# Seven products of halves from block 2 on, with the weights' sums formed in place in block 0's FFN

## The chip, the cores and the metric

The kernel runs on one core of a Trainium2 chip. The metric is the device time of one execution in microseconds (us). Every time below without a unit is in us. Engines: PE is TensorE, DVE VectorE, ACT ScalarE, POOL GpSimd, SP the engine whose queue issues nearly all DMAs.

## The reference

Input x has 4 sequences of 1024 tokens with 512 features. Two layers follow each other, each with a residual and layer norms on both sides:

```
h   = layernorm(x)
q, v, g = h @ Wq.T, h @ Wv.T, silu(h @ Wg.T)          # 512 x 512 each
ret_t = lam * ret_(t-1) + v_t                           # scan over the tokens, lam per head
x   = x + layernorm((layernorm(q * ret) * gamma + beta) * g @ Wo.T)
h   = layernorm(x)
f   = silu(h @ fp8(gate_w) * gate_s) * (h @ fp8(up_w) * up_s)   # 512 -> 1536
x   = x + layernorm(f @ fp8(down_w) * down_s)                   # 1536 -> 512
```

fp8() rounds a weight to float8 e4m3 and back. Everything else is float32. A weight beyond 448 would become a NaN in the reference; the kernel searches for such weights and passes a NaN on if there is one.

## The kernel before, in words

The 4096 tokens are cut into 8 blocks of 512 (NB = 8, TB = 512). Each block goes through a retention part (class Retention) and an FFN part (class Ffn). The two are interleaved: the main loop `for t in range(NB)` runs block t's FFN in NI = 12 steps i. Step i multiplies for the gate (pfg) and for up (pfu), each 8 float32r matmuls of 128x512, forms the fused value, and adds the down product (pd) of step i - 2. Between these groups stand pieces of the retention part of block b = t + 1 and, late in the loop, the first projections of block n = t + 2. At step 11 block n's projections begin; the document calls that place a turn. In the code `a`, `b`, `n` are the retention objects of blocks t, t + 1, t + 2, and `l` is the FFN of block t - 1, whose output norms are finished during this FFN.

The order of the work on each engine is the order of the program text: the wrapper InOrder keeps every instruction in program order on its engine. All instructions are recorded at one line (L74), so groups are told apart by tile names. SP's queue is in order too: a DMA whose input is not ready holds those behind it.

There are two ways to project. Up to block 2 (FAST = 3) the projection is direct: for each of 4 output chunks, 4 matmuls of 128x512 in float32 (pv, pq, pg from wv_sb, wq_sb, wg_sb). A float32 matmul leaves two records in the trace. From block 3 on it is done with seven products of halves (Strassen's scheme): for each of v, q, g seven products of a 256x256 weight quarter (or a sum of quarters) with 256 features of 256 tokens, each 4 matmuls of 128x256 (method product). They need sums of the weight's quarters (operands 5, 6, 7, 3) and sums of the input's quarters (t_sums, formed by input_sums on POOL). The weight operands are fetched from DRAM for each product into w_ring, a ring of 4. The partial results are kept in mids. The three tiles w_ring, t_sums and mids take over the space of wq_sb, wv_sb and wg_sb.

The sums of the weights' quarters are formed in weight_sums on DVE, 12 additions of 128x512 into tiles of the pool work ("tok"), and stored to DRAM by SP (dsum_v, dsum_q, dsum_g), during steps 0 and 1 of block 1's FFN.

Late in each FFN (i = 7 to 11) block b's retention output is finished per slice s of 128 tokens: o (matmul po), o_moments (DVE statistics, POOL reciprocal root), x1_of (normalised x1n, POOL adds it to x, SP stores it as kept), x1_moments, x1n_of, and then the transposed copy x1nT: for s = 0 to 2 by move_x1n, a DVE transpose by blocks and two DMA legs through DRAM (mxs, x1n), and for s = 3 by turn_x1n on TensorE (pt). upper_of (ACT) and rest_of (DVE) write the two halves of x1nT that the next FFN multiplies. For blocks 0 and 1 x1n is computed by ACT (shift_scale), from block 2 on by DVE (center_scale).

The search for weights over 448 (find_over, tile seen) is 24 ACT passes of 128x1536, spread over the steps of block 1's FFN by the list look. Its result is combined in pass_over, with a matmul (over_all) on TensorE, in step 1 of block 2's FFN.

PSUM: pf has two banks for pfg and pfu in turn, pa0 and pa1 serve the retention part, pd0 to pd3 the down sums.

Of the kernel before, what the change touches and what calls it, by code (L numbers as in the profile page):

```python
# [23 lines left out]
def retention_ffn_sandwich(  # L24
# [203 lines left out]
    def find_over():  # L228


        k = 0
        for j in range(4):
            for w in (gate_sb, up_sb, down_sb):
                v = w[:, ts(j, NI // 4), :] if w is down_sb else w[:, :, ts(j, I // 4)]
                for sign in (1.0, -1.0):
                    tag = "ret" if k >= 6 else "xn"
                    seen = work.tile(list(v.shape), F8, tag=tag, name=f"seen_{k}", bufs=2 if k >= 6 else 1)
                    act.activation(
                        seen, v.bitcast(F32), AF.Relu, bias=neg_max, scale=sign,
                        accum_out=over[:, k : k + 1], saturate=False,  # L240
                    )
                    k += 1
                    yield
# [3 lines left out]
    def pass_over():  # L247

        dve.reduce_sum(total, over, mybir.AxisListType.X)
        po = ps_tile("over_all")  # L250
        pe.matmul(po[:, :1], mean_w, total, start=True, stop=True)
        dve.tensor_scalar(total, po[:, :1], 3e38, 3e38, ALU.mult, ALU.mult)
        dve.tensor_scalar(total, total, 0.0, None, ALU.mult)
        dve.tensor_scalar(ds_sb, ds_sb, total, None, ALU.add)


# [72 lines left out]

    FAST = 3  # L330
    H = TB // 2
# [3 lines left out]
    banks = {"v": {1: 0, 6: 1, 5: 0}, "q": {1: 1, 6: 0, 5: 1}, "g": {1: 0, 6: 0, 5: 1}}  # L335
    squares = {"v": (wvT, wv_sb), "q": (wqT, wq_sb), "g": (wgT, lambda: wg_sb)}
    operands = {}

    def weight_sums():

        for k, (src, w) in squares.items():
            w = w() if callable(w) else w
            v = src.rearrange("(c p) f -> p c f", p=P)
            a11, a12, a21, a22 = (w[:, i : i + 2, o : o + H] for o in (0, H) for i in (0, 2))
            operands[k] = {1: v[:, 0:2, 0:H], 2: v[:, 2:4, 0:H], 4: v[:, 2:4, H:D]}
            done = {}
            for j, x, y, op in (
                (5, a21, a22, ALU.add), (6, 5, a11, ALU.subtract),
                (7, a11, a21, ALU.subtract), (3, a12, 6, ALU.subtract),
            ):  # L350
                t = work.tile([P, D], F32, tag="tok", name=f"sum_{k}{j}", bufs=4)
                done[j] = t.rearrange("p (c f) -> p c f", c=2)
                x, y = (done[o] if isinstance(o, int) else o for o in (x, y))
                dve.tensor_tensor(done[j], x, y, op)
                operands[k][j] = dram.tile([P, 2, H], F32, tag=f"sum_{k}{j}", name=f"dsum_{k}{j}", bufs=1)
                sp.dma_start(operands[k][j], done[j])
                yield

    sums = weight_sums()
    RING = 4  # L360
# [478 lines left out]
    for n in range(4):  # L839
        load_piece(n)  # L840
    wg_sb = load_square(wgT, "wg_sb")
    a = Retention(0, x_first)
    a.new_xnT()
# [126 lines left out]

    look = [2, 2, 2, 0, 1, 3, 3, 3, 2, 2, 2, 2]
    l = None
    for t in range(NB):
        f, n = Ffn(a), None
        fast = b is not None and b.fast
        for i in range(NI):
            if t > 0 and (t > 1 or i):
                (f if i else l).rest((i - 1) % NI)
            if t == 0 and i == 0:
                n = Retention(2)  # L980
                rounds(3, now=False)

            if l and i == 0:
                l.fetch()
# [3 lines left out]
            if l and not b and i == 3:  # L988
                for s in range(NS // 2, NS):
                    l.scale(s)  # L990
            if l and b and not fast and i == 3:
                l.norm(0)
                l.add(0)
                l.norm(1)
                l.add(1)
            if l and not b and i in (6, 7):
# [7 lines left out]
            if n and i == 6 and t > 0:  # L1004
                n.stats(2)
                n.stats(3)
                n.rstd()
                if n.fast:
                    n.shift()
            if b and not fast and i == 5:  # L1010
                b.z(0)
            if b and i >= 8:
                b.x1_moments(i - 8)
            f.gate(i)
            if t == 0 and i in (5, 6):
# [5 lines left out]
            if fast and i in (0, 1, 2, 3, 4, 5, 6):  # L1021
                b.product()
            if fast and i == 2:
                l.stats(0)
# [6 lines left out]
            if b and t == 0 and i < 2:  # L1031
                b.q(i + 2, tokens=slice(None) if i else later)
                b.y_of(i + 2)
            if b and not fast and t > 0 and i < 3:
                b.v(i + 1)
                b.scan(i + 1)
            if l and b and not fast and i == 2:
                l.stats(0)
                l.stats(1)
            if b and not fast and i == 3:  # L1040
                b.halves()
                units()
                if t == 0:
                    rounds(3, now=False)
                b.g_of(0)
                b.mean()
                b.center_y()
                if t == 0:
                    n.stats(3)
                    n.rstd()  # L1050
                    n.shift()
            if b and not fast and i == 4:
                b.halves()
                if t == 0:
                    rounds(3, now=False)
                b.g_of(1)
                b.var()
# [3 lines left out]
            if b and not fast and i == 6:  # L1061
                b.g_of(3)
                b.z(2)
                if t == 0:
                    b.z(3)
            if b and 7 <= i <= 10:
# [9 lines left out]
            if b and 7 <= i <= 10:  # L1076
                b.o_moments(i - 7)
            if n and n.fast and i == 11:
                n.input_sums(1, 2)
            units()  # L1080
            f.up(i)
            f.fuse(i)
            if b and not fast and i == 4:
                b.rstd_y()
            if n and i == 11:
                if n.fast:
                    n.products(2)
                else:
                    n.v(0)
                    n.scan(0)  # L1090
                b.turn_x1n(3, "pf")
                b.upper_of(3)
            if fast and i < 6:
                b.product()
            if fast and i == 2:
# [25 lines left out]

            if l and b and not fast and i == 2:
                l.stats(2)
                l.stats(3)
                l.rstd()
# [5 lines left out]
            if l and b and not fast and i == 3:  # L1131
                l.norm(2)
                l.add(2)
                l.norm(3)
                l.add(3)
            if b and not fast and t > 0 and i < 3:
                b.q(i + 1)
                b.y_of(i + 1)
            if b and not fast and i == 6 and t > 0:
                b.z(3)  # L1140
            if n and i == 5 and t == 1:
                n.stats(0)
                n.stats(1)
            if n and i == 6:
# [5 lines left out]
            if n and t > 0 and 6 <= i <= 9:  # L1150
                n.norm_x(i - 6, n.fast)
                n.send_x(i - 6)
# [5 lines left out]
            if b and n and i == 11:  # L1158
                b.rest_of(3)
            if n and i == 11:  # L1160
                if n.fast:
                    n.product()
                    n.input_sums(3, 4)
                else:
                    n.q(0)
                    n.y_of(0)

# [19 lines left out]
            if fast and i == 4:  # L1187
                b.product()
                b.var()
                b.rstd_y()  # L1190
            if n and n.fast and i == 11:
                n.product()
            if n and t > 1 and i == 5:
                n.stats(0)
                n.stats(1)
            if t == 1 and i < 2:
                for _ in range(6):
                    next(sums, None)
            if t == 1 and i == 6:
                t_sums = wpool.tile([P, 4, 2, H], F32, tag="wv_sb", name="t_sums")  # L1200
                w_ring = wpool.tile([P, RING, 2, H], F32, tag="wq_sb", name="w_ring")
                mids = wpool.tile([P, 4, 2, H], F32, tag="wg_sb", name="mids")
                for _ in range(RING):
                    fetch_weights()
            if b and i == 4 and 0 < t < NB - 2:
                n = Retention(t + 2)
            if t == 2 and i == 1:
                pass_over()
            if t == 2 and i == 4:
# [72 lines left out]
```

## Time and profile before

| what | value |
|---|---|
| runs, median of 3 | 992.82 (991.87 to 992.85) |
| the profiled execution | 991.89, span 990.1, granted TensorE clock 0.998 |
| PE busy | 968.6, 98% of the span |
| DVE busy | 657.1, 66% |
| ACT busy | 365.3, 37% |
| POOL busy | 256.4, 26% |
| DMA | 104.56 MB, 106 GB/s in the mean |
| stage of block 0's FFN (95.21 to 201.26) | DVE 80.98, ACT 59.91, DMA share 0.37 at 105 GB/s |
| stage of block 1's FFN (201.26 to 326.04), block 2 direct | PE 122.32 of 124.78, DVE 81.71, ACT 67.05 |
| stage of block 3's FFN (446.03 to 564.80), block 4 by products | PE 117.66 of 118.77, DVE 78.56, ACT 33.95 |

A row of the timeline holds the start, the duration, the engine, the line, the operation, output tile <- input tiles, the shape, how many instructions are merged, and in brackets the idle time of the engine before it with what ended it. A row of the list of waits holds who waited for whom, the sum in us, how many times, and the longest. Matmuls are pipelined and their ends are modelled, so that the distance of two starts is the surer measure.

### The profile page before, as it was taken

How to read it: one execution, taken by the hardware profiler on the slowest of the kernel's cores; microseconds unless marked ns; L12 is line 12 of the kernel's file. 1: busy time of each engine (PE TensorE's matmuls, PEld its weight loads, DVE VectorE, ACT ScalarE, POOL GpSimd, SP SyncE). 2: the span in 40 equal slices, each digit the busy share in tenths (PEclk: the TensorE clock that was granted, in tenths of full speed). 3: DMA queues.
4: the chain of work that ended last, by engine and by line, in shares of the span. 5: the costliest groups of instructions: out<-in, count | busy, mean ns of one | idle time of the engine just before them, and what ended most of it. 6: DMA issues, size and time to landing. Idle time of an engine off the chain costs nothing.

```text
span 990.1 us, 11037 instructions
## 1 busy us (share of the span) xinstructions
PE 968.6 (98%) x3878; PEld 722.0 (73%) x3878; DVE 657.1 (66%) x1006; ACT 365.3 (37%) x549; POOL 256.4 (26%) x337
## 2 busy tenths in 40 slices
PE   9999999999999999999999999999999999999996
PEld 7455766666666878678876788767887788877885
DVE  5996978548746567665686566866567656756445
ACT  3556575433765125221432114321152211512223
POOL 1405121203314033240513305132141312322020
PEclk9999999999999999999999999999999999999999
DMA  9312314412136326253243633245241542213021
GB/s 295 119 64 73 119 64 104 130 64 85 65 98 149 126 69 229 80 144 118 85 128 90 160 91 109 94 129 157 76 149 57 136 138 75 75 32 117 0 86 43
DMA packets 85223, 104.56 MB, mean 106 GB/s; under 512 B 7728, under 2 KB 49712, under 8 KB 85168
## 3 DMA queue, kind: packets, MB, share of 16 engines
q1 hardware_dynamic: 83584, 102.92, 34.5%
q10 hardware_dynamic: 1584, 0.94, 0.5%
q8 instruction: 31, 0.51, 0.2%
q14 instruction: 24, 0.20, 0.1%
HBM read 71.06 MB, written 32.77 MB: 105 GB/s over the span
## 4 chain that ended last, share of the span: by engine, by line
PE 86%; DVE 6%; POOL 3%; ACT 2%; issue 1%; DMA 1%; ACTq 0%; DVEq 0%; SPq 0%; POOLq 0%
PE pfu L74 16%; PE pfg L74 16%; PE pd L74 15%; PE pv L74 10%; PE pg L74 10%; PE pq L74 9%; PE po L74 9%; POOL t_sums L74 1%; DVE st L74 1%; DVE fuse L74 1%; POOL mv L74 1%; DVE scr L74 1%; ACT seen L74 1%; POOL x L74 1%; DVE d L74 1%
## 5 line engine op out<-in xcount | busy, mean ns | idle before, releaser
L74 PE MATMUL pfu<-x1nT,up_sb 128*128 128x512 f32 x768 | 212.1, 418 | 0.0
L74 PE MATMUL pfg<-x1nT,gate_sb 128*128 128x512 f32 x768 | 194.3, 395 | 0.4 <-DVE x1nT L74 0.4
L74 PE MATMUL pd<-down_sb,fuse 128*128 128x512 f32 x720 | 187.2, 401 | 0.0
L74 PEld LDWEIGHTS pfu<-x1nT,up_sb 128*128 128x128 f32 x768 | 144.5, 188 | 44.4 <-issue 14.4
L74 PEld LDWEIGHTS pfg<-x1nT,gate_sb 128*128 128x128 f32 x768 | 144.1, 188 | 30.4 <-DVE x1nT L74 0.8
L74 PEld LDWEIGHTS pd<-down_sb,fuse 128*128 128x128 f32 x720 | 135.3, 188 | 29.3 <-issue 1.7
L74 ACT CAST fuse<-gate 128x512 fp32r<-128x512 f32 x90 | 55.7, 618 | 236.4 <-DVE gate L74 236.4
L74 ACT ACTIVATE gate<-pfg,gs_sb 128x512 f32<-128x512 f32 x96 | 65.7, 684 | 206.2 <-PE pfg L74 206.1
L74 DVE SCALAR_TENSOR_TENSOR gate<-pfu,us_sb,gate 128x512 f32<-128x512 f32 x96 | 71.6, 746 | 82.8 <-PE pfu L74 82.8
L74 PE MATMUL po<-wo_sb,y 128*128 128x512 f32 x256 | 114.5, 592 | 0.0
L74 POOL TENSOR_SCALAR mv<-mv 128x1 f32<-128x1 f32 (+1 forms) x82 | 18.6, 226 | 302.6 <-DVE mv L74 301.6
L74 PEld LDWEIGHTS po<-wo_sb,y 128*128 128x128 f32 x256 | 48.2, 189 | 50.3 <-issue 46.9
L74 DVE TENSOR_TENSOR fuse<-gate,fuse 128x512 fp32r<-128x512 f32 x90 | 75.6, 840 | 9.1 <-ACT fuse L74 9.1
L74 POOL TENSOR_TENSOR ysum<-y 128x256 f32<-128x256 f32 (+1 forms) x13 | 13.5, 1038 | 188.8 <-DVE y L74 161.1
L74 POOL TENSOR_TENSOR x<-x,x1n 128x512 f32<-128x512 f32 x32 | 46.7, 1460 | 45.7 <-DVE x1n L74 36.7
L74 DVE BATCH_NORM_STATS2 st<-x 128x6 f32<-128x512 f32 x64 | 43.6, 681 | 13.7 <-POOL x L74 11.2
L74 DVE TENSOR_TENSOR mids<-pv,mids 128x512 f32<-128x512 f32 x25 | 17.3, 691 | 46.3 <-PE pv L74 43.4
L74 POOL TENSOR_TENSOR mv<-mv,nhalf 128x1 f32<-128x1 f32 (+1 forms) x75 | 45.3, 604 | 6.2
L74 PE MATMUL pv<-xnT,wv_sb 128*128 128x512 f32 (+1 forms) x120 | 42.9, 508 | 1.6 <-ACT xnT L74 1.6
L74 PE MATMUL pv<-t_sums,w_ring 128*128 128x256 f32 x160 | 38.3, 382 | 5.6 <-POOL t_sums L74 5.6
L74 PE MATMUL pq<-xnT,wq_sb 128*128 128x512 f32 (+1 forms) x112 | 43.4, 531 | 0.0
L74 PE MATMUL pg<-xnT,wg_sb 128*128 128x512 f32 x96 | 43.0, 592 | 0.0
(156 smaller groups left out, 1334.5 us busy)
## 6 DMA issues: line engine op xcount, KB each, us to landing
kept<-x SPq DMA_DIRECT2D x32, 256.0 KB, 2.1
x<-kept SPq DMA_DIRECT2D x32, 256.0 KB, 3.7
x<-in_x SPq DMA_DIRECT2D x28, 256.0 KB, 4.1
out<-d SPq DMA_DIRECT2D x27, 256.0 KB, 2.0
xnT<-mx SPq DMA_DIRECT2D x24, 256.0 KB, 4.8
mxs<-xs SPq DMA_DIRECT2D x84, 64.0 KB, 1.8
x1n<-mxs SPq DMA_DIRECT2D x21, 256.0 KB, 2.7
mx<-xn SPq DMA_DIRECT2D x20, 256.0 KB, 2.3
```

Of the source, the lines that this page charges most:

```text
L74: return lambda *args, **kwargs: tc.keep_in_program_order(op(*args, **kwargs))
```

## The change

FAST goes from 3 to 2: block 2 too is projected by seven products. All branches for direct blocks beyond block 1 go away.

The weights' sums are formed earlier and in place. At steps 8, 9 and 10 of block 0's FFN, just ahead of the gate group, DVE makes four additions in wv_sb, then wq_sb, then wg_sb, where the sums overwrite the quarters; at the end of the same step SP stores the four sums. w_ring now takes wv_sb's space and is filled at the end of step 9; t_sums and mids take the others after step 10.

At a turn input_sums forms all four input sums at once before the up group. The products there were 1 and 6, then the transposes, then 2, pd, 7; now they are 1, the transposes, pd, then 6 and 2. Product 7 moves behind the next FFN's first gate group, and step 1 has one product more.

The search runs five passes in steps 0 and 1, four in step 2, two in step 3, none in steps 4 to 6, two in steps 7 to 10 and none in step 11. Its output tile is "xn" for the first 16 passes, "ret" for the others. pass_over becomes a generator of three parts, all in step 0 of block 2's FFN: the sum on DVE ahead of the gate group, the matmul after the first product, the rest on DVE after the up group.

```diff
-                    tag = "ret" if k >= 6 else "xn"
+                    tag = "ret" if k >= 16 else "xn"
...
         dve.reduce_sum(total, over, mybir.AxisListType.X)
-        po = ps_tile("over_all")
+        yield
+        po = ps_tile("over_all", "pa0")
         pe.matmul(po[:, :1], mean_w, total, start=True, stop=True)
+        yield
...
-    FAST = 3
+    FAST = 2
...
+    def weight_sums(k):
+
+        src, w = squares[k]
+        v = src.rearrange("(c p) f -> p c f", p=P)
+        a11, a12, a21, a22 = (w[:, i : i + 2, o : o + H] for o in (0, H) for i in (0, 2))
+        operands[k] = {1: v[:, 0:2, 0:H], 2: v[:, 2:4, 0:H], 4: v[:, 2:4, H:D]}
+        dve.tensor_tensor(a22, a21, a22, ALU.add)
+        dve.tensor_tensor(a21, a11, a21, ALU.subtract)
+        dve.tensor_tensor(a11, a22, a11, ALU.subtract)
+        dve.tensor_tensor(a12, a12, a11, ALU.subtract)
+        return {5: a22, 7: a21, 6: a11, 3: a12}
+
+    def keep_sums(k, done):
+        for j, t in done.items():
+            operands[k][j] = dram.tile([P, 2, H], F32, tag=f"sum_{k}{j}", name=f"dsum_{k}{j}", bufs=1)
+            sp.dma_start(operands[k][j], t)
+
...
-    look = [2, 2, 2, 0, 1, 3, 3, 3, 2, 2, 2, 2]
+    look = [5, 5, 4, 2, 0, 0, 0, 2, 2, 2, 2, 0]
...
+            if t == 2 and i == 0:
+                next(passing)
...
+            if t == 0 and 8 <= i < 11:
+                done = weight_sums("vqg"[i - 8])
             f.gate(i)
...
-            if n and n.fast and i == 11:
-                n.input_sums(1, 2)
+            if n and i == 11:
+                n.input_sums(1, 2, 3, 4)
             units()
             f.up(i)
             f.fuse(i)
...
             if n and i == 11:
-                if n.fast:
-                    n.products(2)
-                else:
-                    n.v(0)
-                    n.scan(0)
+                n.product()
                 b.turn_x1n(3, "pf")
                 b.upper_of(3)
+            if t == 2 and i == 0:
+                next(passing)
             if fast and i < 6:
-                b.product()
+                b.products(2 if i == 1 else 1)
...
+            if t == 0 and 8 <= i < 11:
+                keep_sums("vqg"[i - 8], done)
...
-            if n and n.fast and i == 11:
-                n.product()
+            if n and i == 11:
+                n.products(2)
...
-            if t == 1 and i < 2:
-                for _ in range(6):
-                    next(sums, None)
-            if t == 1 and i == 6:
-                t_sums = wpool.tile([P, 4, 2, H], F32, tag="wv_sb", name="t_sums")
-                w_ring = wpool.tile([P, RING, 2, H], F32, tag="wq_sb", name="w_ring")
-                mids = wpool.tile([P, 4, 2, H], F32, tag="wg_sb", name="mids")
+            if t == 0 and i == 9:
+                w_ring = wpool.tile([P, RING, 2, H], F32, tag="wv_sb", name="w_ring")
                 for _ in range(RING):
                     fetch_weights()
+            if t == 0 and i == 10:
+                t_sums = wpool.tile([P, 4, 2, H], F32, tag="wq_sb", name="t_sums")
+                mids = wpool.tile([P, 4, 2, H], F32, tag="wg_sb", name="mids")
...
-            if t == 2 and i == 1:
-                pass_over()
```

More of the change, by code (lines that the diff above doesn't have):

```diff
@@ L235, in find_over @@
                 for sign in (1.0, -1.0):
-                    tag = "ret" if k >= 6 else "xn"
-                    seen = work.tile(list(v.shape), F8, tag=tag, name=f"seen_{k}", bufs=2 if k >= 6 else 1)
+                    tag = "ret" if k >= 16 else "xn"
+                    seen = work.tile(list(v.shape), F8, tag=tag, name=f"seen_{k}", bufs=2 if k >= 16 else 1)
                     act.activation(
@@ L254, in pass_over @@
         dve.tensor_scalar(ds_sb, ds_sb, total, None, ALU.add)
+        yield
+    passing = pass_over()
     def stats(src, mv):
@@ L335, in retention_ffn_sandwich @@
     banks = {"v": {1: 0, 6: 1, 5: 0}, "q": {1: 1, 6: 0, 5: 1}, "g": {1: 0, 6: 0, 5: 1}}
-    squares = {"v": (wvT, wv_sb), "q": (wqT, wq_sb), "g": (wgT, lambda: wg_sb)}
+    squares = {"v": (wvT, wv_sb), "q": (wqT, wq_sb)}
     operands = {}
[L339 to L359, printed above, removed]
+    def weight_sums(k):
[12 more added lines that the diff above has]
+            sp.dma_start(operands[k][j], t)
     RING = 4
@@ L841, in retention_ffn_sandwich @@
     wg_sb = load_square(wgT, "wg_sb")
+    squares["g"] = wgT, wg_sb
     a = Retention(0, x_first)
@@ L990, in retention_ffn_sandwich @@
                     l.scale(s)
[L991 to L995, printed above, removed]
             if l and not b and i in (6, 7):
@@ L1007, in retention_ffn_sandwich @@
                 n.rstd()
-                if n.fast:
-                    n.shift()
+                n.shift()
             if b and not fast and i == 5:
@@ L1033, in retention_ffn_sandwich @@
                 b.y_of(i + 2)
[L1034 to L1039, printed above, removed]
             if b and not fast and i == 3:
@@ L1042, in retention_ffn_sandwich @@
                 units()
-                if t == 0:
-                    rounds(3, now=False)
+                rounds(3, now=False)
                 b.g_of(0)
@@ L1047, in retention_ffn_sandwich @@
                 b.center_y()
[L1048 to L1051, printed above, removed]
+                n.stats(3)
+                n.rstd()
+                n.shift()
             if b and not fast and i == 4:
                 b.halves()
-                if t == 0:
-                    rounds(3, now=False)
+                rounds(3, now=False)
                 b.g_of(1)
@@ L1063, in retention_ffn_sandwich @@
                 b.z(2)
-                if t == 0:
-                    b.z(3)
+                b.z(3)
             if b and 7 <= i <= 10:
@@ L1082, in retention_ffn_sandwich @@
             f.fuse(i)
-            if b and not fast and i == 4:
+            if t == 0 and i == 4:
                 b.rstd_y()
             if n and i == 11:
-                if n.fast:
-                    n.products(2)
-                else:
-                    n.v(0)
-                    n.scan(0)
+                n.product()
                 b.turn_x1n(3, "pf")
                 b.upper_of(3)
+            if t == 2 and i == 0:
+                next(passing)
             if fast and i < 6:
-                b.product()
+                b.products(2 if i == 1 else 1)
             if fast and i == 2:
@@ L1120, in retention_ffn_sandwich @@
                 next(search)
[L1122 to L1125, printed above, removed]
             if l and not b and i in (4, 5):
@@ L1130, in retention_ffn_sandwich @@
                     l.rstd()
[L1131 to L1143, printed above, removed]
             if n and i == 6:
@@ L1150, in retention_ffn_sandwich @@
             if n and t > 0 and 6 <= i <= 9:
-                n.norm_x(i - 6, n.fast)
+                n.norm_x(i - 6, True)
                 n.send_x(i - 6)
@@ L1159, in retention_ffn_sandwich @@
                 b.rest_of(3)
-            if n and i == 11:
-                if n.fast:
-                    n.product()
[L1163 to L1166, printed above, removed]
+            if t == 0 and 8 <= i < 11:
+                keep_sums("vqg"[i - 8], done)
             if i == f.lag:
@@ L1190, in retention_ffn_sandwich @@
                 b.rstd_y()
-            if n and n.fast and i == 11:
-                n.product()
-            if n and t > 1 and i == 5:
+            if n and i == 11:
+                n.products(2)
+            if n and t > 0 and i == 5:
                 n.stats(0)
                 n.stats(1)
-            if t == 1 and i < 2:
-                for _ in range(6):
-                    next(sums, None)
-            if t == 1 and i == 6:
-                t_sums = wpool.tile([P, 4, 2, H], F32, tag="wv_sb", name="t_sums")
-                w_ring = wpool.tile([P, RING, 2, H], F32, tag="wq_sb", name="w_ring")
-                mids = wpool.tile([P, 4, 2, H], F32, tag="wg_sb", name="mids")
+            if t == 0 and i == 9:
+                w_ring = wpool.tile([P, RING, 2, H], F32, tag="wv_sb", name="w_ring")
                 for _ in range(RING):
                     fetch_weights()
+            if t == 0 and i == 10:
+                t_sums = wpool.tile([P, 4, 2, H], F32, tag="wq_sb", name="t_sums")
+                mids = wpool.tile([P, 4, 2, H], F32, tag="wg_sb", name="mids")
             if b and i == 4 and 0 < t < NB - 2:
                 n = Retention(t + 2)
-            if t == 2 and i == 1:
-                pass_over()
             if t == 2 and i == 4:
```

## The prediction

> **What bounds the kernel now.** I read the page's shares first, then TensorE's list of waits, then the timeline around the points that the change touches. TensorE (PE) is busy nearly all the time; the other engines are not.
>
> ```profile
> PE   968.6 (98%) x3878; PEld 722.0 (73%) x3878; DVE 657.1 (66%) x1006; ACT 365.3 (37%) x549; POOL 256.4 (26%) x337
> ```
>
> So time is won in two ways only: fewer TensorE cycles, or a shorter wait of TensorE. The longest waits in its list:
>
> ```profile
> PE pv L74 <- POOL t_sums L74: 5.6, 5, 1.1
> ...
> PE pv L74 <- DMA mxs<-xs: 1.3, 1, 1.3
> ...
> PE over_all L74 <- DVE total L74: 1.0, 1, 1.0
> ```
>
> All three are touched. The timeline gives the price of the two ways to project. A direct output chunk (8 records of 128x512 f32) and then the same of block 2's stage, and two seven-product steps of a later block:
>
> ```profile
> 203.08 3.59 PE L74 MATMUL pv<-xnT,wv_sb 128*128 128x512 f32 x8
> 206.11 2.39 PE L74 MATMUL pfu<-x1nT,up_sb 128*128 128x512 f32 x8
> 208.34 3.59 PE L74 MATMUL pq<-xnT,wq_sb 128*128 128x512 f32 x8
> ...
> 458.73 1.89 PE L74 MATMUL pq<-xnT,w_ring 128*128 128x256 f32 x8
> 460.27 2.18 PE L74 MATMUL pfu<-x1nT,up_sb 128*128 128x512 f32 x8
> 462.29 1.89 PE L74 MATMUL pq<-t_sums,w_ring 128*128 128x256 f32 x8
> ```
>
> Ends are modelled, so I use starts. A group of the FFN (pfg to pfu, 188.49 to 190.30) takes 1.81. From 203.08 to 208.34 are 5.26, less 1.81 for pfu: 3.45 for a direct chunk. From 458.73 to 462.29 are 3.56, less 1.81: 1.75 for a product.
>
> **Part 1, block 2 by products: TensorE.** Removed are 12 direct chunks, 12 x 3.45 = 41.4; added are 21 products, 21 x 1.75 = 36.75. Gain 4.65. (The whole stages agree: from one pfu_11 to the next, 190.30 to 312.08 are 121.8 with a direct block, 433.82 to 552.42 are 118.6 with a product block, which still contains 1.15 of waits.) What comes with it lies beside TensorE: VectorE is 66% busy in the direct stage (81.71 of 124.78) and in the product stage as well (78.56 of 118.77), so I cost its additions, scans and the 21 weight fetches of 256 KB at nothing; later blocks carry the same load without a TensorE wait in their bodies.
>
> **Part 2, the products at a block's turn are reordered.** Before, product 6 followed product 1 at once and waited for the input sums on POOL. At the end of block 2's FFN, where block 4's products begin (such a place is a turn below):
>
> ```profile
> 435.63 1.89 PE L74 MATMUL pv<-xnT,w_ring 128*128 128x256 f32 x8
> 438.64 1.99 PE L74 MATMUL pv<-t_sums,w_ring 128*128 128x256 f32 x8 [1.12 <-POOL t_sums L74]
> 440.47 0.60 PE L74 MATMUL pt<-ident,x1n 128*128 128x128 f32 x4
> 440.91 1.89 PE L74 MATMUL pv<-xnT,w_ring 128*128 128x256 f32 x8
> ```
>
> From 435.63 to the next pfg at 446.03 are 10.40; four products (7.00), the transposes (0.44) and pd (1.81) need 9.25: 1.15 lost. After the change the order is product 1, transposes, pd, products 6 and 2. The sums end at about 438.58 (POOL 437.26 + 1.32); product 6 comes at 435.63 + 1.75 + 0.44 + 1.81 = 439.6, too late to wait. But the stall goes somewhere: the transposes come 3.1 earlier, at 437.38, and x1n(3) is written on VectorE from 435.99 for 1.47, to 437.46. I leave 0.2 per turn. Four turns (blocks 4 to 7): 4 x 0.95 = 3.8 gained. The turn where block 3's begin loses more, from the end of pfu_11 (312.08 + 1.81 = 313.89) to the next pfg at 326.04 it is 12.15 against 9.25, so 2.9 are lost: there product 1 too waits 1.3, for xnT, which is transposed and fetched late because the ACT norms stand behind three searches (1.57 each by their starts) per step. The search moves from 3 per step at i = 5 to 7 into i = 0 to 3; from i = 7 to 10 two per step stay. In that stretch VectorE's loop ran at 8.75 per step (its gate operation at 292.41, 301.17, 309.92) against TensorE's 8.89, so without the earlier backlog it should keep up. I leave 0.4: gain 2.5.
>
> **Part 3, the search and the check.** Five searches in a step are 7.85 plus gate 0.69 and cast 0.62 = 9.2, under the step's 10.7 (six groups) at i = 0 and 12.4 at i = 1. Behind them queue gate, fuse cast and the copy of product 1, which TensorE needs only a step later. One search at i = 3 stands before the squares; those feed the variance, whose matmul has no slack to show. I charge 0.3, from 0 to 1.5. The over-range check is cut in three: before, 345.82 to 348.88 is 3.06 where a product takes 1.54 of start distance; its own matmul is 0.21, so 1.3 is gained. The VectorE work it then waits for, two scans (1.3), is done before it by TensorE's 3.56 of pfg and a product.
>
> **Part 4, the weights' sums in block 0's FFN, i = 8 to 10: the cost.** Here VectorE runs a loop that is bound by its own chain: statistics of po, gate, ACT's x1n, POOL's add, statistics of x, POOL, ACT's x1n, transposes.
>
> ```profile
> 165.91 0.68 DVE L74 BATCH_NORM_STATS2 st<-x 128x6 f32<-128x512 f32 x1
> 166.63 0.18 DVE L74 BATCH_NORM_AGGREGATE mv<-st 128x2 f32<-128x6 f32 x1
> 168.94 0.71 DVE L74 STREAM_TRANSPOSE xs<-x1n 128x512 f32<-128x512 f32 x1 [2.13 <-ACT x1n L74]
> ```
>
> Four sums go into that gap of 2.13. Chained as they are they take 3 x 0.72 + 0.68 = 2.84 (sum_v: 212.58 to the dependent one at 213.30), so 0.7 per step even if nothing collides. But in the gap POOL must compute the reciprocal root, and this row, where the same POOL operation met a VectorE addition of two SBUF operands, took 1.07 instead of 0.19:
>
> ```profile
> 75.26 1.19 DVE L74 TENSOR_TENSOR gate_sb<-scr 128x1024 fp32r<-128x1024 f32 x1
> ...
> 75.43 1.07 POOL L74 TENSOR_SCALAR mv<-mv 128x1 f32<-128x1 f32 x1 [24.80 <-DVE mv L74]
> ```
>
> The Trainium skill (SBUF — State Buffer, "Who interferes with whom") makes this general: a VectorE instruction with two SBUF inputs and a GpSimd one that reads SBUF exclude each other, and the second to issue waits for the whole first. It speaks against the change: sum 1, POOL's scale, sum 2, POOL's power (0.55), sums 3 and 4 then alternate, and both the sums and x1n end about 1.1 to 1.3 late. By the free gap the three steps cost 2.1, by the rule some 3.6; I take 3.4, nearer the rule, since the row is of this kernel.
>
> x1n(3) is finished at 194.47 before (193.66 + 0.81), so at 197.85 after. TensorE's transposes of it now follow one product instead of a direct chunk: 192.11 + 1.75 = 193.86. Wait: 4.0. From both sides: 2.7 without collisions, 4.5 with all, nothing if the loop absorbs the sums. A part may appear earlier, at pfu_11, which needs the bank that the late gate operation frees; it is the same lateness, not more.
>
> The 12 stores and 4 ring fetches enter SP's queue between the transposing DMAs. Each issue is about 0.33, landing about 2.1 (stores) and 2.7 to 3.2 (fetches). Stores of q and the four fetches go out near 185 and stand in front of block 1's third x1n copy: 2 MB more, about 7 to 9 at the 0.9 to 1.1 per 256 KB that 105 GB/s at 37% DMA share gives. They finish near 193, x1n(2) lands at 197 to 199, beside the wait already charged. The stores of g follow the last kept(3), about 194.5, and land near 199; ACT's first copy into mids waits for them, as mids takes over wg's space. Product 2 needs that copy at 197.85 + 0.44 + 1.81 + 1.75 = 201.85. So I cost the DMAs at nothing, covered by this stall; without it they would cost 1 to 2. Removing the sums from block 1's i = 0 and 1 gains nothing: no TensorE wait stands there.
>
> **Sum.** -4.65 - 3.8 - 2.5 - 1.3 + 0.3 + 4.0 = -7.95. The profiled execution took 991.89 with a span of 990.1; it would be 983.9. The runs' median, 992.82, is 0.9 above it: predicted 984.8.
>
> **Rivals.** (a) *The turn at block 0 is worse.* DMA backlog plus the chain: the copy into mids or x1n(2) comes 3 to 4 after product 2 is ready, or residual waits stay at every turn. For it: 4 MB more through a queue that waits in order; against: DMA share there is 37%. Time 987 to 990. (b) *The loop absorbs the sums.* If collisions are rare and turns close fully: 4.0 falls to between 0.7 and 2.7, residuals to 0: -10.7 to -12.7, or 980 to 982. For it: POOL's power ran beside a VectorE addition unharmed at 161.64; against: the 75.43 row. (c) *Slower: the g stores gate the first copy into mids.* ACT is in order, and behind that copy stand the upper half of x1nT(3) and thus block 1's first pfg. Each microsecond after 201.85 is lost whole; the change turns slower when the stores land after 201.85 + 8 = 209.9, i.e. some 11 later than reckoned. Time from 993 up. Nothing in the trace lands that late except the loads at the start (11.0 for wg_sb). (d) *No difference:* the products gain 4.65, the rest is lost in new waits of the same size: 992 to 993.
>
> **Chances.** Forecast 0.55 (983 to 987), (b) 0.20, (a) 0.18, (c) 0.04, (d) 0.03. The range 980.5 to 989 leaves out the end of (a), (c), (d) and the far end of (b), less than 2 in 10. About 0.2% (2 us) is what a measurement can tell: faster 0.94, same 0.03, slower 0.03.
>
> **What would show it.** Right: pv and pq in block 1's FFN are 128x256 groups of 1.75; no wait for t_sums; over_all without a wait; a wait of pt for x1n of 3 to 4.5 near 194; POOL's mv rows between 166 and 185 stretched to 0.6 or more; x1 transposes at 1 more per step. Wrong: a wait of pv for ACT's mids, a wait of var for half over 1, or pfg waiting for ACT at i = 1 to 2 of block 1.

## The result, and the profile after

The changed kernel takes 985.38 (median of 4 runs, 984.88 to 986.38) where the kernel before takes 992.35 beside it (991.56 to 992.85): ratio 0.9932, interval 0.9915 to 0.9949. A repetition at the end of the study gave 985.26 (5 runs, ratio 0.9926, 0.9914 to 0.9938). It is faster by 7 to 7.6, and the forecast was 984.8. The profiled execution's span went from 990.1 to 983.8.

TensorE's line among the shares of the page, changed kernel:

```profile
PE 964.9 (98%) x3950; PEld 735.9 (75%) x3950; DVE 663.7 (67%) x1019; ACT 369.6 (38%) x556; POOL 265.7 (27%) x346
```

It still bounds the kernel. TensorE's list of waits:

```profile
PE pt L74 <- ACT x1n L74: 2.3, 2, 2.0
...
PE pv L74 <- ACT mids L74: 1.1, 1, 1.1
...
PE pg L74 <- ACT mids L74: 0.6, 1, 0.6
```

The three waits that the prediction set out from (t_sums 5.6, mxs 1.3, over_all 1.0) are gone. Those for mids are new, and that of pt for x1n was 0.3 before. A later turn, at the end of block 2's FFN, in the timeline of the changed kernel:

```profile
433.43 1.89 PE L74 MATMUL pv<-xnT,w_ring 128*128 128x256 f32 x8
435.41 0.63 PE L74 MATMUL pt<-ident,x1n 128*128 128x128 f32 x4
435.80 2.09 PE L74 MATMUL pd<-down_sb,fuse 128*128 128x512 f32 x8
437.73 1.89 PE L74 MATMUL pv<-t_sums,w_ring 128*128 128x256 f32 x8
439.45 1.89 PE L74 MATMUL pv<-xnT,w_ring 128*128 128x256 f32 x8
440.99 2.20 PE L74 MATMUL pfg<-x1nT,gate_sb 128*128 128x512 f32 x8
```

Three products, the transposes and pd need 3 x 1.75 + 0.44 + 1.81 = 7.50 by the prediction's prices; from 433.43 to 440.99 are 7.56, so the turn is closed. (The fourth product now follows pfg.) Block 0's turn in the same timeline is not:

```profile
191.89 1.98 PE L74 MATMUL pfu<-x1nT,up_sb 128*128 128x512 f32 x8
193.71 1.89 PE L74 MATMUL pv<-xnT,w_ring 128*128 128x256 f32 x8
197.64 0.66 PE L74 MATMUL pt<-ident,x1n 128*128 128x128 f32 x4 [2.05 <-ACT x1n L74]
198.05 2.11 PE L74 MATMUL pd<-down_sb,fuse 128*128 128x512 f32 x8
200.00 1.89 PE L74 MATMUL pv<-t_sums,w_ring 128*128 128x256 f32 x8
202.97 1.99 PE L74 MATMUL pv<-xnT,w_ring 128*128 128x256 f32 x8 [1.08 <-ACT mids L74]
204.62 2.20 PE L74 MATMUL pfg<-x1nT,gate_sb 128*128 128x512 f32 x8
```

From the end of pfu (191.89 + 1.81) to pfg are 10.92, where the work needs 7.50. The stall has two parts: the transposes wait for x1n(3), and product 2 for ACT's copy into mids. The cause of the first part, VectorE and then POOL in step 8 of block 0's FFN:

```profile
167.46 2.83 DVE L74 TENSOR_TENSOR wv_sb<-wv_sb 128x512 f32<-128x512 f32 x4
170.47 0.71 DVE L74 STREAM_TRANSPOSE xs<-x1n 128x512 f32<-128x512 f32 x1 [0.18 <-ACT x1n L74]
```

```profile
167.63 0.54 POOL L74 TENSOR_SCALAR mv<-mv 128x1 f32<-128x1 f32 x1 [1.46 <-DVE mv L74]
168.25 1.01 POOL L74 TENSOR_TENSOR mv<-mv,nhalf 128x1 f32<-128x1 f32 x1
```

The four sums take the 2.83 that was reckoned and are not stretched. POOL's two operations are: in the kernel before they take 0.19 and 0.55, so 0.81 more together. x1n is ready only 0.18 after the sums are done (the row at 170.47). The cause of the second part, SP's queue and then ACT:

```profile
185.65 2.88 SPq L74 DMA_DIRECT2D dsum_q<-wq_sb  x4
188.57 0.71 SPq L74 DMA_DIRECT2D w_ring<-in_wvT  x1
...
195.52 0.34 SPq L74 DMA_DIRECT2D x1n<-mxs  x1
...
196.39 2.99 SPq L74 DMA_DIRECT2D dsum_g<-wg_sb  x4
```

```profile
202.33 0.58 ACT L74 COPY mids<-pv 128x512 f32<-128x512 f32 x1 [2.84 <-DMA dsum_g<-wg_sb]
```

A store of a sum takes 0.72 of SP's queue (2.88 for four), not the 0.33 of the prediction; the stores of g are issued from 196.39, and ACT's copy, which may not overwrite wg's space before they have been read, comes at 202.33.

Stretch by stretch, from starts of groups (the turns of the first three rows from the end of pfu at step 11 to the next pfg):

| stretch | before | after | forecast | measured |
|---|---|---|---|---|
| block 0's turn, over the work's 7.50 | (9.15, no loss) | 10.92 | +4.0 | +3.4 |
| turn where block 3's products begin | 12.15, with a fourth product of 1.75 | 7.83 | -2.5 | -2.57 |
| four later turns, each | 10.40, with a fourth product | 7.56 | -3.8 | -4.36 |
| block 2's projections: in block 1's body and block 0's turn | 10 + 2 chunks | 18 + 3 products | -4.65 | -4.3 |
| the search, in block 1's body | | | +0.3 | +0.9 |
| over_all in its step | 3.06 | 1.87 | -1.3 | -1.2 |
| TensorE's clock at half near 131 to 136 | | | not reckoned | +1.6 |

Block 1's body (first pfg to pfu at step 11) went from 110.82 to 109.01. The groups alone would give 10 x 3.45 - 18 x 1.75 = 3.0; measured are 1.81, or 2.70 where two searches are moved away (experiment 7), so 0.9 is the search, and the projections have 2.7 there and, by the prices, 1.65 at the turn (9.15 against 7.50). The measured terms add up to -6.5, the spans differ by 6.3.

### The profile page after: what moved, and what is told of

It reads as the page before. It is cut to its first block, busy times and chain, and to the rows that moved or that the text cites. A ratio compares the mean times of both kernels' runs of the same rounds, so it can differ in the third digit from the quotient of the medians.

```text
span 983.8 us, 11259 instructions
## 1 busy us (share of the span) xinstructions
PE 964.9 (98%) x3950; PEld 735.9 (75%) x3950; DVE 663.7 (67%) x1019; ACT 369.6 (38%) x556; POOL 265.7 (27%) x346
## 4 chain that ended last, share of the span: by engine, by line
PE 82%; DVE 9%; ACT 4%; POOL 2%; issue 1%; DMA 1%; SPq 0%; ACTq 0%; DVEq 0%; POOLq 0%
PE pfu L74 15%; PE pfg L74 15%; PE pd L74 15%; PE pv L74 10%; PE pq L74 9%; PE pg L74 9%; PE po L74 8%; DVE st L74 2%; DVE scr L74 1%; POOL mv L74 1%; POOL x L74 1%; DVE fuse L74 1%; ACT x1n L74 1%; DVE gate L74 1%; DVE xs L74 1%
## 5 line engine op out<-in xcount | busy, mean ns | idle before, releaser
L74 PE MATMUL pg<-t_sums,w_ring 128*128 128x256 f32 x192 | 45.7, 381 | 0.6 <-ACT mids L74 0.6
L74 PE MATMUL pv<-t_sums,w_ring 128*128 128x256 f32 x192 | 45.3, 379 | 0.0
L74 PE MATMUL pq<-t_sums,w_ring 128*128 128x256 f32 x192 | 45.3, 379 | 0.0
L74 PEld LDWEIGHTS pg<-t_sums,w_ring 128*128 128x128 f32 x192 | 35.9, 189 | 7.3 <-ACT mids L74 2.1
L74 PEld LDWEIGHTS pv<-t_sums,w_ring 128*128 128x128 f32 x192 | 36.3, 189 | 5.7
```

Source lines behind the costliest of these rows:

```text
L74: return lambda *args, **kwargs: tc.keep_in_program_order(op(*args, **kwargs))
```

## The experiments

**1. The order at the turns alone.** The kernel before, with the new order at the turns and the check in three parts (that edit is as in the change, and left out here); block 2 direct, the sums and the search at their old places.

```diff
-                n.input_sums(1, 2)
+                n.input_sums(1, 2, 3, 4)
...
-                    n.products(2)
+                    n.product()
...
-                b.product()
+                b.products(2 if i == 1 else 1)
...
-                n.product()
+                n.products(2)
```

> The kernel before with only the order of products at a turn and the split of the over-range check taken from the change; block 2 stays direct, the sums and the search stay where they were. Theory 1 (the gain is the waits at the turns, block 2's own products are paid back at block 0's turn): four turns of 1.09, 1.2 at the turn of block 3, 1.2 at the check: -6.8, a ratio near 0.993, within 1.5 us of the changed kernel. Theory 2 (block 2's 21 products bring the gain of 4.65): -2 to -3 only, a ratio of 0.997 to 0.998.

Measured: 985.89 (984.42 to 987.06), ratio 0.9938 (0.9926 to 0.995), span 985.3. Nearly the whole gain is there without a product more. In this kernel the four turns are 7.57, the check costs as little, and block 3's turn keeps a wait:

```profile
317.13 1.97 PE L74 MATMUL pv<-xnT,w_ring 128*128 128x256 f32 x8 [1.14 <-DMA mxs<-xs]
```

That turn is 9.16 against 7.83. Block 0's turn is 9.16 and block 1's body 110.81, as before the change. So by rows, block 2's products, with all that they bring in the changed kernel, are worth -1.8 in block 1's body and +1.8 at block 0's turn (10.92): nothing. Of the difference between the two spans, 1.5, block 3's turn is 1.33. The medians of the runs differ less, and their intervals overlap.

**2. The old order at the turns, the rest of the change kept.** The edits shown in experiment 1, undone in the changed kernel; the check stays in three parts.

> The changed kernel with the old order at a turn: two input sums, products 1 and 6, transposes, product 2, pd, product 7, the other two sums. Theory (the reorder is worth the wait for t_sums): waits of pv for t_sums are back at 5 turns, 1.1 each, 5.4 in all; block 0's turn is ruled by x1n(3) and the stores of g in either order, so it loses less than 1; time +5 to +6 against the changed kernel, ratio 0.998 to 0.999. Rival (the waits move to pt or to the next pfg when product 6 is later, so the reorder only shifts them): within 2 of the changed kernel, ratio 0.993 to 0.995.

Measured: 995.27 (993.07 to 996.6, 12 runs), ratio 1.0029 (1.002 to 1.0038): slower than before the change, by more than forecast. TensorE's waits:

```profile
PE pv L74 <- POOL t_sums L74: 9.0, 6, 3.4
...
PE pv L74 <- DVE total L74: 1.0, 1, 1.0
```

The longest, of 3.4, is at block 0's turn (199.14), which is a turn of products now too; the five others are of the old kind. Block 0's turn is 16.81 with its fourth product of 1.75, which is 4.1 more than in the changed kernel where less than 1 was expected. (The clock is halved in it, 0.50 from 202 to 206.) The second wait is that of a product at 337.30, behind the check's matmul; it was not foreseen. The reorder is what carries the change.

**3. The sums left out.** The 12 additions of VectorE are not executed; their stores and all else stay.

```diff
-        dve.tensor_tensor(a22, a21, a22, ALU.add)
-        dve.tensor_tensor(a21, a11, a21, ALU.subtract)
-        dve.tensor_tensor(a11, a22, a11, ALU.subtract)
-        dve.tensor_tensor(a12, a12, a11, ALU.subtract)
```

> The changed kernel without the 12 additions (the raw quarters are stored in their place, so q, v and g of blocks 2 to 7 are wrong). Theory 1 (VectorE's chain at i = 8 to 10 is late by the sums): the steps fall from 9.3 to 8.5, the wait of pt for x1n falls to about 0.6, the time falls by 2 to 2.5 against the changed kernel, ratio 0.990 to 0.991. The wait of product 2 for mids stays at 1 or more, as the stores stay. Theory 2 (the 16 transfers in SP's queue make the wait): pt waits as before, ratio 0.993.

Measured: 987.69 (986.39 to 988.77), ratio 0.9954 (0.994 to 0.9968). With less work it is slower, against the expectation. Block 0's turn in this kernel:

```profile
203.37 3.17 PE L74 MATMUL pv<-xnT,w_ring 128*128 128x256 f32 x8 [3.65 <-ACT mids L74]
```

The wait for x1n(3) is gone (0.3), as expected, but product 2 is now ready earlier and waits for the copy into mids, which comes no earlier (202.73, against 202.33 in the changed kernel): the stores of g go out at 196.84, there at 196.39, so they do not depend on VectorE's lateness. And the product itself takes 3.17, since the clock is halved after the wait. The turn is 12.39.

**4. Statistics in place of the sums.** As many VectorE operations of about the same length (2.44 for four against 2.83), with one operand in SBUF instead of two; the weights' sums are not formed.

```diff
-        dve.tensor_tensor(a22, a21, a22, ALU.add)
...
+        for c in range(NC):
+            st = small.tile([P, 6], F32, tag="st", name="st2")
+            dve.bn_stats(st, w[:, c, :])
```

> The changed kernel with each of the 12 additions replaced by statistics over 128x512 of the same weight: one SBUF input, 0.69 each, so VectorE is as busy, but no two-input instruction meets POOL (the sums are left out, outputs of blocks 2 to 7 are wrong). Theory 1 (two delays lie side by side in a step: 0.7 of VectorE's own time and 0.8 of POOL's stretched root): POOL's two rows are back at 0.19 and 0.55, but steps stay near 9.2 and pt waits within 0.4 of the changed kernel. Theory 2 (the two delays add, as predicted): steps fall to 8.7 or below and the time falls by 1.3 or more.

Measured: 987.84 (985.29 to 987.93), ratio 0.9952 (0.9939 to 0.9964). The time is spoilt by the same wait for mids (3.57 at 202.05, then a product of 3.78). But POOL's rows beside the statistics tell what was asked:

```profile
166.22 0.19 POOL L74 TENSOR_SCALAR mv<-mv 128x1 f32<-128x1 f32 x1 [1.46 <-DVE mv L74]
166.49 0.56 POOL L74 TENSOR_TENSOR mv<-mv,nhalf 128x1 f32<-128x1 f32 x1
```

They are not stretched, and VectorE has no idle time left in the gap:

```profile
166.05 2.44 DVE L74 BATCH_NORM_STATS2 st<-wv_sb 128x6 f32<-128x512 f32 x4
168.40 0.69 DVE L74 STREAM_TRANSPOSE xs<-x1n 128x512 f32<-128x512 f32 x1
```

A step of VectorE's loop is 8.63 (statistics of x at 165.23 and 173.86) against 8.51 before and 9.31 with the sums. x1n(3) ends at 194.17, before at 194.47 (block 0 begins 0.6 earlier here). The steps speak for the second theory, the time for neither. The lateness of 0.8 a step in the changed kernel is POOL's, held up beside the additions. That the sums would fit into the gap is not shown, as they are 0.39 longer than the statistics: from the rows of step 8 (sums done near 170.2; x1n, without POOL's 0.81, ready at 169.66) I estimate that they alone would cost about 0.5 a step. Nor is it isolated that the second SBUF operand does it: the statistics also write less, 6 numbers a row instead of 512.

**5. Two of the four early fetches one step later**, so that the stores of g are issued sooner.

```diff
-                for _ in range(RING):
+                for _ in range(2):
                     fetch_weights()
             if t == 0 and i == 10:
+                for _ in range(2):
+                    fetch_weights()
```

> The changed kernel with two of the four first ring fetches moved from the end of step 9 to the end of step 10, behind the stores of g. Theory 1 (the copy into mids waits because SP issues the stores of g late, behind the fetches and the x1n copy that waits for its mxs): stores of g start 0.9 earlier, the wait of pv for mids falls from 1.1 to 0.3 or less, time -0.5 to -1 unless product 2 then waits for its own fetch. Theory 2 (the bytes in the DMA rings, not SP's order, set the landing): the wait stays at 1.

Measured: 985.01 (984.28 to 987.7), ratio 0.9934 (0.9921 to 0.9947): no difference that counts. The stores go out at 194.44 instead of 196.39, the copy into mids comes at 200.33 instead of 202.33, and product 2 does not wait; but the transposes wait 2.50, and a clock drop follows. That drop limits what this run can say. In the repetition of the unchanged kernel the transposes wait 2.49, the clock drops too, and product 2, late by the drop, comes at 202.55 without a wait although the copy comes at 201.87. The two turns are 11.74 and 11.79. So experiments 3 and 4 show that lifting the first limit alone gives nothing, since the second then holds product 2 for 3.6; that lifting the second alone gives nothing was measured only together with a drop.

**6. An earlier wait on the same chain.** In step 4 of block 0's FFN the variance's matmul, which waits 1.4 near 130, is put behind the up group.

```diff
                 b.g_of(1)
+                f.up(i)
                 b.var()
...
-            f.up(i)
+            if not (t == 0 and i == 4):
+                f.up(i)
```

> The changed kernel with one move on TensorE alone: in block 0's step 4 the variance's matmul goes behind the up group, so that the wait of var for half (1.4) ends. Theory 1 (VectorE's chain through block 0's FFN, not TensorE, sets when x1n(3) is there): TensorE is 1.4 earlier at step 5 and pt waits that much longer, 3.5 to 4.5; the time stays within 0.7 of the changed kernel. The granted clock shows no 0.50 near 131 to 135 (if a wait of 1.4 is what can halve it). Theory 2 (TensorE sets the turn): -1.4 or more.

Measured: 984.86 (984.68 to 985.7), ratio 0.9926 (0.9914 to 0.9938), the same time. The wait is gone at 130 and reappears 1.3 long at 143.61 and 2.5 long at block 0's turn, as long as in the repetition without this edit: VectorE's chain sets that turn, not the matmuls ahead of it.

**7. The search.** Two searches of block 1's FFN moved from step 3 to steps 5 and 6; and in another kernel the old plan and its old buffers.

```diff
-    look = [5, 5, 4, 2, 0, 0, 0, 2, 2, 2, 2, 0]
+    look = [5, 5, 4, 0, 0, 1, 1, 2, 2, 2, 2, 0]
```

> The changed kernel with the two searches of block 1's step 3 moved to steps 5 and 6, after the fuse cast. Theory (the search at step 3 stands before the squares and product 1 of g's reader on ACT): the wait of pg for ACT's mids, 0.6, ends; time -0.6 to -0.8, ratio 0.992 to 0.993, and no new wait at the turn of block 3. Rival: the wait comes from POOL's and VectorE's order and stays.

Measured: 984.7 (984.43 to 985.4), ratio 0.9923 (0.9911 to 0.9936). That is 0.6 to 0.7 lower, which the runs alone cannot tell, but block 1's body is 108.12 against 109.01. Of these two rows of the changed kernel and of this one, at the same place, the first starts behind a wait and the second doesn't:

```profile
254.28 1.99 PE L74 MATMUL pg<-t_sums,w_ring 128*128 128x256 f32 x8 [0.61 <-ACT mids L74]
```

```profile
253.38 1.91 PE L74 MATMUL pg<-t_sums,w_ring 128*128 128x256 f32 x8
```

> The changed kernel with the search's old plan (three in a step at steps 5 to 7 of block 1's FFN) and its old buffers. Theory (the search's plan gives the turn of block 3 its gain): pv's wait for xnT of about 1.3 is back at that turn, the turn is longer by 1 to 1.8, the wait of pg for mids (0.6) near 254 is gone; the time is 0.7 to 1.5 above the changed kernel. Rival (the reordering of the turn alone gave that gain): the turn stays at 7.8 to 8.2, and the time is 0.3 to 0.7 below.

Measured: 987.65 (986.01 to 990.02), ratio 0.9952 (0.9938 to 0.9965), 2.4 above the changed kernel beside it; 0.7 to 1.5 were expected. The turn of block 3 is 9.23, with its wait back:

```profile
315.91 1.97 PE L74 MATMUL pv<-xnT,w_ring 128*128 128x256 f32 x8 [1.35 <-DMA xnT<-mx]
```

That gives +1.4. Block 1's body is 109.54 against 109.01, since the wait for mids is missing but another comes that I had not foreseen, of po for y at 276.93 (1.16): by rows +1.9 in all. (The profiled execution is the fastest of the six and free of clock drops, so its span, 984.1, does not show the difference.) So of the 2.57 gained at block 3's turn about half is the order (experiment 1: 12.15 less 1.75 against 9.16, which is 1.24) and half the search's plan.

**8. Spreading the sums.** From here on I looked for a better place. Per loop step one sum stands behind the loop's second half, and two ahead of the gate operation, behind a small VectorE copy that waits for POOL's root and so keeps the additions off it; the three sums that are left over, of v, stand in step 6. (some_sums(n) makes the next n of the twelve; rounds(n) does the next n pieces of the rounding of the FFN weights.) With it go the moved searches and fetches of experiments 5 and 7.

```diff
-                done = weight_sums("vqg"[i - 8])
+                dve.tensor_copy(total, b.mvo[i - 8][:, 1:2])
+                some_sums(2)
...
+                if i == 6:
+                    rounds(1, now=False)
+                    some_sums(3)
+                    rounds(2, now=False)
...
+                if 8 <= i < 11:
+                    some_sums(1)
```

> The changed kernel with the 12 additions spread: three in step 6 in a VectorE gap without POOL, then per step one right after the fuse rest and two after POOL's root is done (a 128x1 copy that waits for it); stores follow in the same steps; two ring fetches at step 9 and two at step 10; the two searches as in the run with steps 5 and 6. Theory (the sums' lateness of 0.8 per step and SP's order make block 0's turn): POOL's root rows are 0.19 and 0.55, steps 8.7 or less, pt waits 1.3 or less, no wait for mids; time -2 to -2.8 against the changed kernel, ratio 0.9905 to 0.9915. Rival (a wait for a store or a fetch takes its place): within 1 of the changed kernel.

Measured: 985.86 (985.2 to 987.0), ratio 0.9934 (0.9922 to 0.9946): nothing gained, though POOL's rows are back at 0.19 and 0.55 and the wait for mids is gone. The transposes still wait 2.56. Step 6 has no gap on VectorE: the three sums (156.71, 2.14 long) shift everything behind them. The gap is one step earlier: in the changed kernel the addition into scr at 148.48 stands idle for 2.04, waiting for ACT. (The clock is halved twice in this execution, near 132 and near 200.)

**9. The same with the three sums in step 5**, and once more with the edit of experiment 6.

```diff
-                if i == 6:
+                if i == 5:
```

> The additions are spread again, now into gaps that the trace shows: the three remaining sums of v stand in step 5 of block 0's FFN, where VectorE has a gap of 2.0 before a gate operation that waits for ScalarE (it was empty in the run with step 6), the sums of q and g in twos ahead of the gate operation and in ones behind the second half of the loop; the searches at steps 5 and 6 and the two late fetches stay. Theory 1 (VectorE's lateness at steps 8 to 10 sets block 0's turn): pt's wait for x1n falls from 2.0 to between 0 and 1.2, the first pfg of block 1 comes 1 to 2 earlier, the time is 1 to 2.5 below the changed kernel, 983 to 984.5. Theory 2 (the wait is replaced by the next one: mids, xnT or the stores): a wait of 1 or more appears at the same turn and the time stays within 0.7 of the changed kernel.

> The changed kernel once more, on the same chip as the three others of this call, for their differences: 985.0 to 986.0; 0.993 of the kernel before.

Measured: 982.04 (981.77 to 982.87), ratio 0.9894 (0.9881 to 0.9907); the changed kernel beside it 985.26, ratio 0.9926 (0.9914 to 0.9938). This beats both kernels, by 10.9 and 3.2. VectorE in step 8 of this kernel, then TensorE at block 0's turn:

```profile
168.09 0.15 DVE L74 COPY total<-mv 128x1 f32<-128x1 f32 x1 [0.95 <-POOL mv L74]
168.16 0.68 DVE L74 TENSOR_TENSOR wv_sb<-wv_sb 128x512 f32<-128x512 f32 x1
168.76 0.69 DVE L74 TENSOR_TENSOR wq_sb<-wq_sb 128x512 f32<-128x512 f32 x1
169.36 0.71 DVE L74 STREAM_TRANSPOSE xs<-x1n 128x512 f32<-128x512 f32 x1
```

```profile
196.18 0.66 PE L74 MATMUL pt<-ident,x1n 128*128 128x128 f32 x4 [0.97 <-ACT x1n L74]
196.59 2.09 PE L74 MATMUL pd<-down_sb,fuse 128*128 128x512 f32 x8
198.52 1.89 PE L74 MATMUL pv<-t_sums,w_ring 128*128 128x256 f32 x8
200.25 1.89 PE L74 MATMUL pv<-xnT,w_ring 128*128 128x256 f32 x8
201.79 2.20 PE L74 MATMUL pfg<-x1nT,gate_sb 128*128 128x512 f32 x8
```

The turn is 8.47 (201.79 less 191.51 + 1.81), 2.45 shorter than in the changed kernel, and block 1's body is 108.15, 0.86 shorter, which the moved searches gave in experiment 7 too: 3.3 of the 3.9 between the two spans. The copy into mids comes at 198.07 and nothing waits for it. Neither limit holds the turn for long any more; the later fetches and the spread sums were not run apart in this version. Against experiment 1, block 0's turn and block 1's body are together 3.35 shorter (8.47 + 108.15 against 9.16 + 110.81): once the sums lie well, block 2's products do pay.

> The same as the kernel with the sums in step 5, and in step 4 of block 0's FFN the variance's matmul stands behind the up group, so TensorE doesn't wait 1.4 there. In the other run with this edit the clock stayed whole near 131 and the wait went to the next places of VectorE's chain. If with the spread sums VectorE's chain isn't the limit any more, the time is 1 to 2 below the kernel with the sums in step 5; if VectorE is still the limit at the turn, it is the same within 0.5.

Measured: 982.77 (981.07 to 983.64), ratio 0.9898 (0.9885 to 0.9911), no better. The transposes wait 2.08 there, and the clock drops in the turn (0.50 from 198 to 200), which is 11.15: VectorE's chain is still the limit. From block 0's first pfg to block 1's, where an early and a late drop both count, it is 106.98 without this edit and 107.77 with it, against 109.38 in the changed kernel and 108.91 in its repetition.

## Why the prediction was right, and where not

The total was right within 0.6 (984.8 against 985.38), inside the forecast's own range; what it was made of was partly wrong, and that it came so close is in part luck. Block 0's turn cost 0.6 less than forecast, and the four later turns together 0.6 less; the search cost 0.6 more and the projections 0.3 more, and the clock, which was not in the sum, 1.6. By the profiled spans the gain is 6.3 where 7.95 was forecast, by the medians 7.0 to 7.6; the profiled execution of the kernel before had no clock drop and lay 0.9 below the median that the forecast started from.

- *The turns and the check:* the mechanism and the sizes held. The residual of 0.2 a turn was too careful (0.06), the 0.4 at block 3's turn about right (0.33).
- *Block 2 by products:* 4.3 of the 4.65. It is a gain that block 0's turn takes back, which the sum said (-4.65 and +4.0); experiment 1 shows how completely.
- *The loop at steps 8 to 10:* the wait came where it was forecast, but the reckoning took it that VectorE's sums and POOL's operations alternate and that both end 1.1 to 1.3 late. Only POOL's operations are stretched; the sums run on, and the two delays lie side by side. The step costs the longer one, 0.8. The "0.7 per step even if nothing collides" is nearer 0.5 by the estimate under experiment 4, and it is hidden behind POOL's. In the repetition, whose clock was whole up to the turn, x1n(3) ended at 196.82, 2.35 late; 3.4 were forecast.
- *"So I cost the DMAs at nothing, covered by this stall"* failed. The copy into mids was reckoned possible at 199 and needed at 201.85; it came at 202.33, and product 2 lost 1.08. The mis-sized number is the issue of stores and fetches, taken as 0.33 for every DMA: the stores of g were to go out at 194.5 and be issued in 4 x 0.33, and went out at 196.39, behind slower stores and fetches, and took 2.99. (With two fetches fewer ahead of them they go out at 194.44, experiment 5.) The trace of before has the same stores, four in 2.57:

```profile
227.92 2.57 SPq L74 DMA_DIRECT2D dsum_g<-sum_g  x4
```

- At this turn a first wait of 4.0 was forecast and by starts 2.2 came (193.71 + 1.75 to 197.64); a second of 1.2 came that was not forecast (200.00 + 1.75 to 202.97). The two errors nearly cancel. Rival (c) named the mechanism of the second at about a seventh of the size at which it would have decided (1.2 lost, where 8 were needed); rival (b), the loop absorbs the sums, is what experiment 9 comes near to by other places for them: block 0's turn loses 0.97 there, within that rival's 0.7 to 2.7.
- *The search* was charged 0.3 within a bound of 1.5, and cost 0.9.
- *The clock* was not in the sum; see the last section.
- *The signs:* of those for right, the groups of 1.75, the ends of the waits for t_sums and over_all and POOL's longer rows came (0.54 and 1.01 for 0.19 and 0.55); the wait of pt was 2.05, 2.49 in the repetition, instead of 3 to 4.5. Of those for wrong, pv's wait for mids came. That of var for half is 1.36, but it was 1.37 before.

Left open: in the better version steps 9 and 10 of the loop are still 9.13 and 9.16 long against 8.52 and 8.53 before; POOL's addition to x is stretched there from 1.27 to 1.67 and 1.70, with a VectorE addition beside it. That was seen in the trace and not tried.

## What to carry to other kernels

Where a stage ends at two waits for different chains, taking away one buys nothing, and the run that takes it away can even look like proof that it did not matter; read which wait comes next, and lift both. A gap on VectorE was not free for additions of two SBUF operands, because POOL operations of the chain fell into it: put such additions behind POOL's result, not beside it. A DMA's time in the queue is read from the same kind of transfer in the trace, not from the commonest one.

## What the hardware showed unexpectedly

TensorE's clock drops to half for a few microseconds after a short wait, and not in every execution. The changed kernel and its repetition, behind the variance's wait of 1.36 and 1.37, first the one and then the other:

```profile
131.50 3.19 PE L74 MATMUL pfu<-x1nT,up_sb 128*128 128x512 f32 x8
```

```profile
131.50 2.00 PE L74 MATMUL pfu<-x1nT,up_sb 128*128 128x512 f32 x8
```

The same group starts at the same time. The granted clock by stretches of 2, of the first and of the second (the first number is TensorE's busy time, the one ahead of the DMA share the clock):

```profile
132.00:134.00 2.00, 2.00 (x6) 1.59 (x5) 1.97 (x2) 1.96 (x4) 0.00 (x0) 0.50 0.00 0
134.00:136.00 2.00, 2.00 (x7) 1.56 (x6) 1.36 (x3) 1.57 (x2) 0.00 (x0) 0.65 0.30 81
```

```profile
132.00:134.00 2.00, 2.00 (x10) 1.65 (x9) 1.97 (x2) 1.96 (x4) 0.00 (x0) 1.00 0.00 0
...
198.00:200.00 2.00, 2.00 (x6) 1.59 (x5) 1.08 (x2) 0.89 (x2) 2.00 (x3) 0.50 1.02 345
```

The second has its drop at block 0's turn instead, behind a wait of 2.49. Of the fourteen profiled executions only those of the kernel before and of the old search have neither (mean clock 0.998, although the old search waits 2.5 at that turn as well); three have both. Twelve have the variance's wait of 1.4, and in seven of them the clock drops behind it; the two that have it taken out (experiment 6 and the last one) keep the clock there. A drop costs about 1.6: TensorE reaches block 0's last pfu at 191.89 with it and at 190.55 without it, and of the latter 0.27 were waited ahead of that pfu (188.47 to 190.55 are 2.08, where 1.81 is usual). The Trainium skill (TensorE: Matmul & The Clock Gate, part 1, on the clock gate) says that the activity is watched in a free-running window of some 3.4, which would fit that it depends on the execution; but the same page's rule in "HAM oscillation", that idle gaps over about 3.4 are to be avoided, doesn't cover waits of 1.4 and 2.5. What decides between the two places was not tested. For the reading it means that single traces of two kernels differ by 1.6, or twice that where one has both drops, for no reason of theirs, so that a term of this size is read from its own rows and not from spans.

The lock between VectorE and GpSimd that the Trainium skill describes (SBUF — State Buffer, "Who interferes with whom") showed more narrowly than I had taken it: beside the sums POOL's operations of 0.19 and 0.55 took 0.54 and 1.01, and the sums, 2.83 for four, stayed as they were. Beside a long POOL operation VectorE is the one held up: its product for fuse, 0.69 at 173.31, takes 1.76 at 164.96, next to POOL's addition to x (1.49 from 164.69).
